# Reordering the front of a fused convolution and attention kernel

## The chip, the cores and the metric

The kernel runs on one core of one Trainium2 chip. All data is float32. The metric is the device time of one launch in microseconds (us); the table below has the median of three runs.

## The reference

The input x has 8 images of 512 channels and 32 x 32 pixels. Cut to what matters:

```python
x = x + block(group_norm(x, 32 groups, eps 1e-5))

def block(x):
    t = silu(bn(conv1x1(x, cv1_w)))                # 512 -> 512 channels
    ys = [t[:, :256], t[:, 256:]]                  # y0 and y1
    for i in range(2):
        yi = ys[-1]
        z = silu(bn(conv3x3(yi, m_cv1_w[i])))      # 256 -> 256
        q, k, v = split(conv1x1(z, m_qkv_w[i]))    # 4 heads of 64
        z = softmax(q^T (k + rw + rh) / 8) applied to v
        ys.append(yi + silu(bn(conv1x1(z, m_cv2_w[i]))))
    return silu(bn(conv1x1(concat(ys), cv2_w)))    # 1024 -> 512
```

The 3x3 convolution is computed in a transformed domain in both directions: filters are turned into "powers" (sums of taps, `make_u`), images into tile inputs (`tiles_in`), products are taken on TensorE, and the results are summed back on VectorE (`conv3x3`).

## The kernel before

**Tiling.** Channels lie on the 128 partitions, so an image of x is four parts (`xts[0]` to `xts[3]`) of 128 x 1024, and the first convolution cv1 has four output blocks of 128 channels: blocks 0 and 1 are y0, blocks 2 and 3 are y1. `Y_ORDER` is 2, 3, 0, 1, because y1 is what the 3x3 convolution needs. Images are worked in pairs; the first pair is called A and B here. Everything that the change touches lies in the front, which is the work ahead of and inside the first 3x3 convolution.

**Norm.** `group_norm_part` is a generator with three steps. The first takes the mean and variance of each channel, either on VectorE (`gn_stats`: two bn_stats and an aggregate for a part) or on ScalarE (`stats_by_act`: a sum by Identity, then a sum of squares by Square, both over 1024 elements). The second averages the mean over groups of 16 channels with a small matmul (`gn_mean`, product gm_ps). The third averages the variance (`gn_rstd`, product gv_ps), raises it to -1/2 with a power on GpSimd (POOL, L700), forms the shift on POOL (L736, L737) and lets ScalarE apply scale and shift in place (L743). Image A is split in two halves: parts 0 and 1 by VectorE, parts 2 and 3 by ScalarE. Image B (`xs_second`) is done by ScalarE as a whole.

**Filters.** `make_u(n, oc, k, area, ...)` makes the powers of one filter block from its nine taps. It goes through i = 2, 0, 1; each i has six VectorE operations of 256 elements (L411 to L416), two ScalarE copies (L409, L410), and for i = 0 and 1 three more VectorE operations of 384 elements ahead (L393 to L399). For output block 0 of the first filter both k go into nine tiles of their own (`first_units`, tag "u", a ring of ten), which the convolution uses directly; when k = 1 is done they are stored to DRAM as nine 512 KB transfers. The two k of block 1 go through twelve half buffers of tag "pt" as eighteen stores of 256 KB. All stores are issued by POOL at L420. The behind_u callback puts some of these steps between applications of B's norm.

**Tile inputs.** `tiles_in(yp, put, is_, ec)` makes the inputs for i = 0, 1 and 2 from y1 of one image. It needs the silus of blocks 2 and 3 (L463). For each i it makes row sums (L520, L524, L527 and L535 to L542), column differences (L556, L557) and the tiles v_in (L559 to L567); POOL writes two edge columns of w_rows (L529, L530). `v_units` places v_in: i = 0 and 1 take the six "pt" buffers, i = 2 takes "v", which held cv1's weights (`w1_first`), and one "x" buffer. Both images share each v_in tile, so a convolution unit starts when both images have written it.

**Order.** Each engine runs its own instructions in one fixed order. A planner forms that order from the order of the program as priority, from dependences and from its own estimates of time, so an instruction written later can come earlier on a free engine. `tc.issue_after(ins)` holds the instructions of a block behind `ins` where both are on the same engine; it makes no wait between engines. Products of cv1 begin before an image's norm is whole: `begin(oc, ks)` runs the parts `ks` of a block and keeps the accumulator in `begun`. There are three accumulators of two banks (`ps_big`), so a fourth block waits until ScalarE's silu has emptied one.

The lines of the front that set this order, before:

```python
begin(Y_ORDER[0], [1])
first = begin(Y_ORDER[1], [0])
with tc.issue_after(first.ins):
    multiplied, _, applied, shifted = next(norm)       # image A, parts 2 and 3
...
s.cv1(w1_of, xs, y0s, Y1[0], Y_ORDER, begun)           # image A
...
s.cv1(w1_of, xs_second, y0s, Y1[1], Y_ORDER)           # image B
```

## Time and profile before

| | us |
|---|---|
| three runs, median (lowest to highest) | 2297.32 (2295.73 to 2301.26) |
| profiled execution, its own time | 2295.83 |
| span in the profile, first to last instruction | 2294.2 |
| TensorE busy over the span | 2217.6 |
| VectorE busy over the span | 1755.7 |
| ScalarE busy over the span | 1090.1 |
| end of the first 3x3 convolution's sums on VectorE | 133.9 |

A timeline line gives the start in us from the span's start, the time taken, the engine (PE is TensorE, DVE VectorE, ACT ScalarE, POOL GpSimd), the line of the kernel, the operation, the tile written and the tiles read, the shape and how many instructions are merged. In brackets is how long the engine stood idle ahead of it, and what ended that. A line of the wait list gives the waiting instruction, what it waited for, and the total, the number and the longest. A line of windows gives busy time by engine, then the granted TensorE clock, the busy share of the DMA engines and GB/s. An f32 matmul appears as two records.

### The profile page before, as it was taken

The page shows a single profiled execution, that of the slowest core. Times are in us where ns is not written, and L with a number is a line of the kernel's source. Part 1 is how long each engine was busy: PE and PEld are TensorE (multiplying, and loading weights), DVE is VectorE, ACT ScalarE, POOL GpSimd, SP SyncE. Part 2 cuts the span into 40 slices and gives each one's busy share as a digit, 9 for nine tenths or more (in the row PEclk, how much of TensorE's full clock was granted, in tenths as well). Part 3 has the DMA queues.
Part 4 walks back from the last instruction along what each step waited for, and adds up shares of the span by engine and source line. Part 5 has one row for each costly group of instructions (what it writes and reads, how often), then busy time and mean ns, then how long its engine had stood idle before and what let it go on. Part 6 is the DMA issues. An engine that isn't in the chain of part 4 may idle for free.

```text
span 2294.2 us, 40531 instructions
## 1 busy us (share of the span) xinstructions
PE 2217.6 (97%) x16338; PEld 1083.3 (47%) x16338; DVE 1755.7 (77%) x2706; ACT 1090.1 (48%) x1342; POOL 208.6 (9%) x417
## 2 busy tenths in 40 slices
PE   6899999999999999999999999999999999999997
PEld 2553437443465443734347443554345733473443
DVE  7887889778858689886857868986894868886742
ACT  7245462545225666365323665445622455335533
POOL 4012200000120000000021000000012000000003
PEclk9999999999999999999999999999999999999999
DMA  9533626321474232612158141442126611251114
GB/s 336 195 108 111 257 76 232 117 75 63 104 221 146 77 123 89 215 44 92 52 150 267 33 160 49 161 132 75 57 73 176 223 46 49 70 196 40 50 28 135
DMA packets 127892, 281.06 MB, mean 123 GB/s; under 512 B 34096, under 2 KB 55324, under 8 KB 126672
## 3 DMA queue, kind: packets, MB, share of 16 engines
q1 hardware_dynamic: 99712, 192.25, 25.4%
q0 software_dynamic: 27984, 86.13, 12.3%
q8 instruction: 131, 2.15, 0.4%
q14 instruction: 65, 0.53, 0.1%
HBM read 210.29 MB, written 68.03 MB: 121 GB/s over the span
## 4 chain that ended last, share of the span: by engine, by line


## 5 line engine op out<-in xcount | busy, mean ns | idle before, releaser
L986 ACT ACTIVATE pt<-l_ps 128x1024 f32<-128x1024 f32 x512 | 495.3, 1023 | 354.5 <-PE l_ps L982 321.8
L1002 DVE TENSOR_TENSOR acc<-acc,pt 128x1024 f32<-128x1024 f32 x384 | 469.6, 1223 | 95.1 <-ACT pt L986 71.3
L1016 PE MATMUL av_ps<-pt,vT 64*64 64x512 f32 x4096 | 489.2, 595 | 11.0 <-DVE z L1024 10.7
L982 PE MATMUL l_ps<-q,kr 64*64 64x512 f32 x4096 | 486.7, 591 | 2.9 <-ACT pt L986 1.9
L1016 PEld LDWEIGHTS av_ps<-pt,vT 64*64 64x64 f32 x4096 | 155.9, 133 | 285.9 <-issue 240.4
L982 PEld LDWEIGHTS l_ps<-q,kr 64*64 64x64 f32 x4096 | 158.1, 133 | 272.9 <-issue 250.6
L611 PEld LDWEIGHTS c_ps<-v_in,u 128*64 128x64 f32 x4320 | 235.7, 137 | 5.3 <-issue 5.3
L611 PE MATMUL c_ps<-v_in,u 128*64 128x128 f32 x4320 | 237.5, 273 | 0.0
L616 ACT COPY c_m<-c_ps 128x512 f32<-128x512 f32 x48 | 28.1, 584 | 185.3 <-PE c_ps L611 108.7
L1214 PE MATMUL m_ps<-z,m_sb 128*128 128x512 f32 x256 | 112.5, 592 | 0.0
L872 PE MATMUL p_ps<-t_z,sq 128*128 128x512 f32 x224 | 106.7, 595 | 3.1 <-DVE c_t L633 3.1
L1000 DVE TENSOR_TENSOR acc<-pt 128x1024 f32<-128x1024 f32 x64 | 77.9, 1217 | 39.2 <-ACT pt L986 39.2
L463 ACT ACTIVATE t<-m_ps,bh,sh 128x512 f32<-128x512 f32 x64 | 46.4, 773 | 75.8 <-PE m_ps L1214 75.8
L872 PE MATMUL p_ps<-z,sq 128*128 128x512 f32 x168 | 80.7, 604 | 0.4 <-ACT m_z L909 0.4
L1284 POOL DMA_DIRECT2D c_out<-in_x_dram x56 | 50.4, 991 | 313.1 <-ACT c_out L463 310.8
L1214 PEld LDWEIGHTS m_ps<-z,m_sb 128*128 128x128 f32 x256 | 48.3, 190 | 58.8 <-issue 56.0
L1088 DVE TENSOR_TENSOR z<-z,rs 128x512 f32<-128x512 f32 x64 | 43.8, 685 | 20.7 <-DMA rs<-r_dram 20.3
L463 ACT ACTIVATE c_out<-cz,bh,sh 128x512 f32<-128x512 f32 x14 | 16.7, 1292 | 90.2 <-DVE cz L1311 90.2
L1024 DVE TENSOR_TENSOR z<-av_ps,z 128x512 f32<-128x512 f32 x64 | 44.0, 688 | 19.7 <-ACT z L1023 19.7
L463 ACT ACTIVATE z<-z,bh,sh 128x512 f32<-128x512 f32 x64 | 47.8, 805 | 21.4 <-DVE z L660 21.4
L490 PE MATMUL ps<-x,w 128*128 128x512 f32 x128 | 56.1, 595 | 0.0
L1334 PE MATMUL x_ps<-t_x,sw 128*128 128x512 f32 x128 | 55.9, 592 | 0.0
(322 smaller groups left out, 3146.2 us busy)
## 6 DMA issues: line engine op xcount, KB each, us to landing
u<-u SPq DMA_DIRECT2D x135, 512.0 KB
sq<-sq SPq DMA_DIRECT2D x42, 384.0 KB
rs<-r_dram SPq DMA_DIRECT2D x118, 128.0 KB
x<-in_x_dram SPq DMA_DIRECT2D x28, 512.0 KB
r_in<-r SPq DMA_DIRECT2D x28, 512.0 KB
y_in<-y SPq DMA_DIRECT2D x28, 512.0 KB
c_out<-in_x_dram POOLq DMA_DIRECT2D x56, 256.0 KB, 5.3
out_dram<-c_out POOLq DMA_DIRECT2D x56, 256.0 KB, 3.7
```

Of the source, the lines that this page charges most:

```text
L463: silued[0] = nc.scalar.activation(dst, src, AF.Silu, scale=sh[:, k : k + 1], bias=bh[:, k : k + 1])
L490: last_product[0] = nc.tensor.matmul(ps[:, half, :], w_of(k), rhs_of(k, half), start=(k == begin), stop=(k == end))
L611: nc.tensor.matmul(to[o], us[cp][:, k, row, c, o], rhs, start=(k == 0), stop=(k == NM - 1),)
L872: nc.tensor.matmul(ps[:, o, :], w[:, o, :], rhs, start=not onto, stop=True, skip_group_check=onto)
L982: nc.tensor.matmul(ps[kh * HD : (kh + 1) * HD, hd, :], kr[r, c, o : o + HD], q[r, c, ts(half, HALF)], start=True, stop=True,)
L986: last_exp[0] = exp = nc.scalar.activation(pt, ps, AF.Exp, scale=SCALE)
L1000: return nc.vector.tensor_tensor(accs[g], pt[0], pt[1], ALU.add)
L1002: ins = nc.vector.tensor_tensor(accs[g], accs[g], pt[i], ALU.add)
L1016: nc.tensor.matmul(avs[g][hd * HD : (hd + 1) * HD, kh, :], vT[r, j, o : o + HD], pt[i][r, hd, :], start=(j == 0), stop=(j == NJ - 1),)
L1214: nc.tensor.matmul(pss[half][:, oc, :], m2_sb[:, n, k, ts(oc, P)], ao[:, k, ts(half, HALF)], start=(k == 0), stop=(k == NM - 1),)
L1284: nc.gpsimd.dma_start(t, rows_of(x, i, at), accum_op=ALU.add)
L1334: nc.tensor.matmul(ps[:, o, :], w[:, c, ts(o, P)], rhs[c], start=(c == 0 and not onto), stop=(c == 1), skip_group_check=onto,)
```

## The change

For image A's second half, the first of two filter steps stays ahead of the variance read and the second goes behind it; block 3 takes both of its first parts before that read. The shift of every such norm is one VectorE operation (`stt`) instead of two on POOL. `make_u` can collect its stores in a list: those of the first unit (`first_stores`) are issued after image B's power and in the program behind the tile inputs, and those of the second filter's beginning (`kept_back`) right after B's power. Image B's statistics use ScalarE for three parts and VectorE for the fourth, and are split in two steps: image A's silus of block 2 stand between the sums and the sums of squares, and those of blocks 3 and 0 behind the squares, ahead of the application of B's norm. Block 1 of image A is computed around B's mean and variance products, and its silus follow the application. Image B's products take parts 0 and 1 of blocks 2 and 3 first. Tile inputs are ordered: image A i = 0 and 1, image B i = 0 and 1, then i = 2 of each. For this pair, i = 2 takes tags "p3" and "p4" instead of "v". The small copies `turn_r` are put behind B's last silu, and in the attention behind an exp.

```diff
--- before.py
+++ after.py
@@ -383,7 +383,7 @@
     def u_new_late():
         return ring([P, 2, 2, P], "u_new")
 
-    def make_u(n, oc, k, area, full=None, new=u_new_late):
+    def make_u(n, oc, k, area, full=None, new=u_new_late, stores=None):
 
         raw = area[:, : 9 * P].rearrange("p (r c o) -> p r c o", r=3, c=3)
         mid = area[:, 9 * P : 15 * P].rearrange("p (r c o) -> p r c o", r=2, c=3)
@@ -417,8 +417,16 @@
             if not full or k == NM - 1:
                 for cp in range(3):
                     dst = u_dram[n][oc][i][cp]
-                    nc.gpsimd.dma_start(dst if full else dst[:, k], full[i, cp] if full else us[cp])
+                    to = (dst, full[i, cp]) if full else (dst[:, k], us[cp])
+                    if stores is None:
+                        nc.gpsimd.dma_start(*to)
+                    else:
+                        stores.append(to)
             yield last
+
+    def put_stores(stores):
+        while stores:
+            nc.gpsimd.dma_start(*stores.pop(0))
 
     NSUM = B * N * NM * NH
     QP = 2 * HALF // P
@@ -465,7 +473,7 @@
             )
             return silued[0]
 
-        shifted, k_added = [None], []
+        shifted, powered, k_added = [None], [None], []
         silu_in, last_product, silued, last_exp, m2_silu = [], [None], [None], [None], [None]
 
         def exp_table():
@@ -697,7 +705,7 @@
             ins = over_groups(ps, dev)
             gr = small.tile([P, n], F32, tag="gr", name="gr")
             read = nc.vector.tensor_scalar(gr, ps, GN_EPS, None, ALU.add)
-            nc.gpsimd.tensor_tensor(gr, gr, mhalf[:, :n], ALU.pow)
+            powered[0] = nc.gpsimd.tensor_tensor(gr, gr, mhalf[:, :n], ALU.pow)
             return gr, ins, read
 
         def stats_by_act(mv, xts):
@@ -707,34 +715,32 @@
             mean = small.tile([P, n], F32, tag="gm", name="mean")
             square = small.tile([P, n], F32, tag="dev", name="square")
 
-            def each(func, to, **kw):
-                for c in range(n):
+            def each(cs, func, to, **kw):
+                for c in cs:
                     bias = {k: v[:, c : c + 1] for k, v in kw.items()}
                     junk = act.tile([P, HW], F32, tag="acc", name="junk", bufs=2)
                     nc.scalar.activation(junk, xts[c], func, accum_out=to[:, c : c + 1], **bias)
 
-            each(AF.Identity, total)
+            each(range(n), AF.Identity, total)
             nc.scalar.activation(mean, total, AF.Identity, scale=-1.0 / HW)
-            each(AF.Square, square, bias=mean)
-            nc.scalar.activation(mv[:, :, 0], total, AF.Identity, scale=1.0 / HW)
-            nc.scalar.activation(mv[:, :, 1], square, AF.Identity, scale=1.0 / HW)
-
-        def group_norm_part(xts, by_act=False, behind=lambda c: None):
+            yield
+            each(range(n), AF.Square, square, bias=mean)
+            nc.scalar.activation(mv[:, :n, 0], total, AF.Identity, scale=1.0 / HW)
+            return nc.scalar.activation(mv[:, :n, 1], square, AF.Identity, scale=1.0 / HW)
+
+        def group_norm_part(xts, by_act=0, behind=lambda c: None):
 
             n = len(xts)
             mv = small.tile([P, n, 2], F32, tag="mv", name="mv", bufs=2)
-            if by_act:
-                stats_by_act(mv, xts)
-            else:
-                for c in range(n):
-                    gn_stats(mv, c, xts[c])
-            yield
+            for c in range(by_act, n):
+                gn_stats(mv, c, xts[c])
+            counted = (yield from stats_by_act(mv, xts[:by_act])) if by_act else None
+            yield counted
             gm, dev, averaged = gn_mean(mv, n, ps_av, "av")
             yield averaged
             gr, multiplied, read = gn_rstd(dev, n, ps_av, "av")
             shift = small.tile([P, n], F32, tag="dev", name="shift")
-            nc.gpsimd.tensor_tensor(shift, gm, gr, ALU.mult)
-            shifted = nc.gpsimd.tensor_scalar(shift, shift, -1.0, None, ALU.mult)
+            stt(shift, gm, -1.0, gr, ALU.mult, ALU.mult)
             for c in range(n):
                 ahead = behind(c)
                 for half in range(NH):
@@ -743,7 +749,7 @@
                         applied = nc.scalar.activation(
                             part, part, AF.Identity, scale=gr[:, c : c + 1], bias=shift[:, c : c + 1]
                         )
-            yield multiplied, read, applied, shifted
+            yield multiplied, read, applied, powered[0]
 
         def group_norm(xts, pieces=1):
 
@@ -1199,8 +1205,8 @@
         def cv1(w_of, xts, y0s, y1, ocs, begun={}):
 
             for oc in ocs:
-                ks = range(NX // 2 if oc in begun else 0, NX)
-                ps = cv1_products(w_of, xts, oc, ks, begun.get(oc))
+                ps, at = begun.get(oc, (None, 0))
+                ps = cv1_products(w_of, xts, oc, range(at, NX), ps)
                 for half in range(NH):
                     dst = y0s[half][:, oc, :] if oc < NM else inner(y1, oc - NM, half)
                     silu(planes(dst), natural(ps[:, half, :]), bn_cv1 + oc)
@@ -1503,17 +1509,19 @@
             nc.sync.dma_start(y1s[half].rearrange("p h c w -> p (h c w)"), y1_dram[b][:, ts(half, NM * HALF)])
         return [[img2(y0s[half]), y1s[half].rearrange("p h c w -> p c h w")] for half in range(NH)]
 
-    def v_units():
+    def v_units(first=False):
 
         vs = {}
         for i in range(NI):
-            if i == 2:
+            if i == 2 and first:
+                both = [act.tile([P, 2, G, 2 * P], F32, tag=tag, name="v_in") for tag in ("p3", "p4")]
+            elif i == 2:
                 both = act.tile([P, 2, 2, G, 2 * P], F32, tag="v", name="v_in")
             for cp in range(3):
                 if i < 2:
                     vs[i, cp] = act.tile([P, 2, G, 2 * P], F32, tag="pt", name="v_in", bufs=6)
                 elif cp < 2:
-                    vs[i, cp] = both[:, cp]
+                    vs[i, cp] = both[cp] if first else both[:, cp]
                 else:
                     vs[i, cp] = act.tile([P, 2, G, 2 * P], F32, tag="x", name="v_in", bufs=NX)
         return vs
@@ -1535,9 +1543,9 @@
                 next(chunk)
         return copied_u[0] if c else None
 
-    first_units = {}
+    first_units, kept_back, first_stores = {}, [], []
     _, _, (_, read, applied, _) = s.group_norm_part(xs[: NX // 2])
-    norm = s.group_norm_part(xs[NX // 2 :], by_act=True)
+    norm = s.group_norm_part(xs[NX // 2 :], by_act=NX // 2)
     for i in (2, 0, 1):
         for cp in range(3):
             first_units[i, cp] = ring([P, NM, 2, 2, P], "u_new")
@@ -1546,11 +1554,13 @@
         for _ in range(5):
             made = next(chunk)
     with tc.issue_after(applied.ins):
-        next(norm)
+        for _ in range(2):
+            next(norm)
     begun = {}
 
     def begin(oc, ks):
-        begun[oc] = s.cv1_products(w1_of, xs, oc, ks, begun.get(oc))
+        ps, _ = begun.get(oc, (None, 0))
+        begun[oc] = s.cv1_products(w1_of, xs, oc, ks, ps), ks[-1] + 1
         return s.last_product[0]
 
     with tc.issue_after(made.ins):
@@ -1559,25 +1569,22 @@
     first = begin(Y_ORDER[0], [0])
     with tc.issue_after(first.ins), tc.issue_after(made.ins):
         averaged = next(norm)
-    chunk = make_u(0, 0, 1, areas[0, 0, 1], first_units)
+    chunk = make_u(0, 0, 1, areas[0, 0, 1], first_units, stores=first_stores)
     with tc.issue_after(averaged.ins):
-        for _ in range(2):
-            made = next(chunk)
+        made = next(chunk)
     begin(Y_ORDER[0], [1])
-    first = begin(Y_ORDER[1], [0])
-    with tc.issue_after(first.ins):
-        multiplied, _, applied, shifted = next(norm)
+    begin(Y_ORDER[1], [0])
+    first = begin(Y_ORDER[1], [1])
+    with tc.issue_after(first.ins), tc.issue_after(made.ins):
+        multiplied, _, applied, powered = next(norm)
     with tc.issue_after(multiplied.ins):
-        begin(Y_ORDER[1], [1])
         begin(Y_ORDER[2], range(NX // 2))
-    with tc.issue_after(made.ins), tc.issue_after(shifted.ins):
+    with tc.issue_after(made.ins), tc.issue_after(powered.ins):
         nc.vector.tensor_scalar(rstd, bnp[:, :, 3], BN_EPS, None, ALU.add)
         nc.gpsimd.tensor_tensor(rstd, rstd, mhalf[:, :NBN], ALU.pow)
-        for _ in range(3):
+        for _ in range(4):
             made = next(chunk)
-    with tc.issue_after(made.ins), tc.issue_after(applied.ins):
-        norm = s.group_norm_part(xs_second, by_act=True, behind=behind_u)
-        next(norm)
+    with tc.issue_after(made.ins):
         for made in chunk:
             pass
     with tc.issue_after(made.ins):
@@ -1587,34 +1594,56 @@
 
         for at in bn_m1:
             made = nc.vector.tensor_scalar(sh[:, at : at + NM], sh[:, at : at + NM], 1 / 36, None, ALU.mult)
-    chunk = make_u(0, 1, 0, areas[0, 1, 0], new=u_new_early)
+    y0s = new_y0()
+    norm = s.group_norm_part(xs_second, by_act=NX - 1, behind=behind_u)
+    with tc.issue_after(applied.ins), tc.issue_after(made.ins):
+        next(norm)
+    s.cv1(w1_of, xs, y0s, Y1[0], Y_ORDER[:1], begun)
+    with tc.issue_after(s.silued[0].ins):
+        counted = next(norm)
+    with tc.issue_after(counted.ins):
+        s.cv1(w1_of, xs, y0s, Y1[0], Y_ORDER[1:3], begun)
+    chunk = make_u(0, 1, 0, areas[0, 1, 0], new=u_new_early, stores=kept_back)
     with tc.issue_after(made.ins):
         for _ in range(4):
             made = next(chunk)
-    with tc.issue_after(made.ins):
+    first = begin(Y_ORDER[3], [0, 1])
+    with tc.issue_after(made.ins), tc.issue_after(first.ins):
         averaged = next(norm)
-        multiplied, _, applied, shifted = next(norm)
-    with tc.issue_after(averaged.ins), tc.issue_after(shifted.ins):
+    first = begin(Y_ORDER[3], [2])
+    with tc.issue_after(made.ins), tc.issue_after(s.silued[0].ins), tc.issue_after(first.ins):
+        multiplied, _, applied, powered = next(norm)
+    with tc.issue_after(powered.ins):
+        put_stores(kept_back)
+    with tc.issue_after(averaged.ins), tc.issue_after(powered.ins):
         for made in chunk:
-            pass
+            put_stores(kept_back)
         for made in make_u(0, 1, 1, areas[0, 1, 1], new=u_new_early):
             pass
-    y0s = new_y0()
-    s.cv1(w1_of, xs, y0s, Y1[0], Y_ORDER, begun)
-    with tc.issue_after(shifted.ins):
+    with tc.issue_after(multiplied.ins):
+        begin(Y_ORDER[3], [3])
+    with tc.issue_after(applied.ins):
+        s.cv1(w1_of, xs, y0s, Y1[0], Y_ORDER[3:], begun)
+    with tc.issue_after(powered.ins):
         keep_y(0, y0s, Y1[0])
     for n in range(N):
         load_m2(n)
     y0s = new_y0()
-    s.cv1(w1_of, xs_second, y0s, Y1[1], Y_ORDER)
-    vs = v_units()
+    begun = {}
+    for oc in Y1S:
+        begun[oc] = s.cv1_products(w1_of, xs_second, oc, range(NX // 2)), NX // 2
+    s.cv1(w1_of, xs_second, y0s, Y1[1], Y_ORDER, begun)
+    vs = v_units(first=True)
+    last = None
     with tc.issue_after(made.ins):
         ecs = [{}, {}]
-        for i in range(NI):
-            for g in range(G):
-                last = s.tiles_in(Y1[g], putter(vs, g), [i], ecs[g])
-    turn_r(0, rw_raw)
-    with tc.issue_after(last.ins):
+        for g, is_ in ((0, (0, 1)), (1, (0, 1)), (0, (2,)), (1, (2,))):
+            with tc.issue_after(last.ins) if last else nullcontext():
+                last = s.tiles_in(Y1[g], putter(vs, g), is_, ecs[g])
+    with tc.issue_after(s.silued[0].ins):
+        turn_r(0, rw_raw)
+    with tc.issue_after(powered.ins):
+        put_stores(first_stores)
         keep_y(1, y0s, Y1[1])
     for (i, cp), u in first_units.items():
         fed["u", 0, 0, i, cp] = u
@@ -1677,7 +1706,7 @@
 
         feed(units(0) + (direct_keys(0) if direct else sqs(0, 0)))
         if p == 0:
-            with tc.issue_after(shifted.ins):
+            with tc.issue_after(powered.ins):
                 first_taps, second_taps = [load_late(0, k, inside(Y2[k])) for k in range(NM)]
         z = new_z()
         t = s.conv3x3(0, vs, u_of(0), z, summed=None if direct else z[:, :, 0], after=last_out)
@@ -1752,7 +1781,8 @@
             raw_1 = load_r(1)
 
             def with_r():
-                turn_r(1, raw_1)
+                with tc.issue_after(s.last_exp[0].ins):
+                    turn_r(1, raw_1)
                 make_r(1)
                 first()
 
```

## The prediction

> **What bounds the kernel now.** The page first: TensorE is busy for 97% of the span, but its first slices read 6, 8, 9, so the loss is at the front. Then the wait lists of VectorE, TensorE and ScalarE between 0 and 160 us, then the timelines of the same engines, then windows.
>
> ```profile
> PE 2217.6 (97%) x16338; PEld 1083.3 (47%) x16338; DVE 1755.7 (77%) x2706; ACT 1090.1 (48%) x1342; POOL 208.6 (9%) x417
> ...
> DVE w_ba L520 <- ACT ypad L463: 8.4, 1, 8.4
> DVE taps L397 <- ACT u_new L410: 1.5, 1, 1.5
> DVE u_new L414 <- DMA u<-u_new: 1.2, 1, 1.2
> DVE dev L692 <- ACT mv L720: 0.9, 1, 0.9
> ...
> 71.18 1.23 DVE L520 SCALAR_TENSOR_TENSOR w_ba<-ypad 128x1024 f32<-128x1024 f32 x1 [8.42 <-ACT ypad L463]
> ```
>
> The reader is to see that VectorE's front is one nearly closed row of work (filter powers, tile inputs, convolution sums) until 133.5 us, and that after 31 us it has one large hole: 62.8 to 71.2, where it waits for image B's first y1. From 71.2 it hardly stops until the convolution ends, while TensorE waits for it (7.7 us at 103.1). So before 133.5 the kernel ends when VectorE ends; after it TensorE leads. Only what fills that hole, or takes VectorE work away, moves the end. Now why image B is late:
>
> ```profile
> 38.89 0.54 POOL L420 DMA_DIRECT2D u<-u_new  x1 [1.55 <-DMA u<-u_new]
> 41.01 0.54 POOL L420 DMA_DIRECT2D u<-u_new  x1 [1.58 <-DMA u<-u_new]
> 41.57 1.27 POOL L700 TENSOR_TENSOR gr<-gr,mhalf 128x4 f32<-128x4 f32 x1
> ...
> 43.79 2.93 ACT L743 ACTIVATE x_second<-x_second,shift,gr 128x512 f32<-128x512 f32 x4 [2.65 <-POOL shift L737]
> ...
> 51.27 2.20 ACT L463 ACTIVATE ypad<-ps,bh,sh 128x512 f32<-128x512 f32 x2
> ...
> 53.52 29.12 PE L490 MATMUL ps<-x_second,w_first 128*128 128x512 f32 x64 [5.19 <-ACT ypad L463]
> ...
> 40.00:60.00 20.00, 13.62 (x28) 5.89 (x29) 17.03 (x40) 15.64 (x26) 13.02 (x23) 0.91 1.02 388
> ```
>
> The power of B's norm is ready to run at 39.6 (its input ends then on VectorE) but stands in POOL's queue behind filter stores that wait for earlier stores to land, and starts at 41.57. ScalarE then applies the norm before it empties image A's products, so TensorE has no free accumulator and starts B at 53.5. The last row says that the DMA engines are full (1.02) at 388 GB/s.
>
> **The change, part by part.**
>
> *Image A's second half.* One filter step instead of two ahead of the variance read takes three VectorE operations (about 1.0 us at 0.335 each) off the path; without stores ahead, the power starts about 1 us earlier again; VectorE's shift (a 0.16 us operation, like L692) replaces 0.67 us of POOL. B's statistics begin on ScalarE about 2 us earlier, near 27. On VectorE nothing gets shorter: it is full from 20.8 to 31.4.
>
> *Image B's statistics.* Part 3 moves to VectorE: two bn_stats and one aggregate, 1.29 + 0.21 = 1.5 us added to the bounding engine; two shifts add 0.4 with their gaps. ScalarE loses 1.04 + 1.13 and their reads.
>
> *When B is ready.* TensorE has 14 pieces (one channel block by one input part, four matmul records of 0.43, so 1.72 us) ahead of B's mean: 12.4 + 14 x 1.72 + about 2 for slow starts is 38.7. One piece more and the variance product: 40.9, which is later than now (39.1). With the power at once (1.27) and the shift, ScalarE applies from about 43.0, hardly earlier than 43.8. The real shift is that the six silus of blocks 2, 3 and 0 (1.1 each) are already done, with statistics and silus filling 27 to 43. Accumulators are free, B's products begin at about 44 on parts 0 and 1, parts 2 and 3 are applied by 49.6, and blocks 2 and 3 (8 pieces, 13.8 us) end at 57.6. Their silus end near 60, against 71.15 now.
>
> *Tile inputs.* Image A's i = 0 and i = 1 now come before B's. A's i = 1 costs 5.1 us (its operations in 77.9 to 89.8, halved, less what belongs to i = 2). Filter powers end at 55.2 now; A then has 6.3 (i = 0) + 1.2 (two L524) + 5.1 = 12.6 us, to about 68. B is ready at 60, so VectorE never waits: the 8.42 goes, with 8 us of margin on B's side. Image B could even slip to 68 at no price.
>
> *The filter waits.* 1.54 + 1.15 + 0.94 = 3.6 us now. I put 2.0 for what replaces them: six stores held until 42.6 mean that the second filter's buffers return a little late (0.5 to 1), and its third step still waits for ScalarE's copies behind the norm (about 1). Bounds 0 and 4. The VectorE shift waits for POOL's power with the queue behind it; the stall is 0 if other filter work stands ahead, 1.3 for the whole power. It lies in these bounds.
>
> *Held stores.* Nine of 512 KB and the six of 256 KB leave POOL's queue ahead of the powers and come after 42.6 with the twelve remaining filter stores (3.1 MB), image A's y (2.1 MB) and two loads of 1.2 MB. POOL pays nothing new: each issue is 0.54 as before. But DMA is nearly idle from about 27 to 42.6 and full after. The risk is the buffers "pt": the inputs of i = 1 take those of the last filter stores. VectorE wants them at about 66. If all 12.7 MB go first at 388 GB/s, they land at 42.6 + 32.7 = 75; if filter stores go first, at about 60. The trace: a 256 KB store lands after 6.3 us median and the longest filter store took 12.5, in a full queue; issued at 57 that is 63.3 or 69.5. The Trainium skill, DMA: Bandwidth & Descriptors, Anatomy of one DMA, speaks for the gentler end: 2.0 us plus bytes over 436 GB/s, an estimate of 2.6 us, landing at 59.6 and waiting nothing. By the rule the sum is 8.1, by the longest row 4.6. The trace decides against the rule while queues are full; I take the median row, with 0.5 us of wait, because program order puts filter stores before the first unit's. Ends 0 and 9.
>
> *TensorE's clock.* Windows after the 5.19 us hole show 0.73, then 0.50 in 54 to 56. The Trainium skill, TensorE: Matmul & The Clock Gate, Part 1, says that an idle window of about 3.4 us halves the clock until a busy one has passed. Without that hole B's products would save some 1.7 us by the rule, making the sum 9.3. I add nothing: VectorE, not B's products, sets the end, and the new wait ahead of the convolution (B's products end near 72, tile inputs of i = 0 at 75.6) would cool the clock again.
>
> *The rest.* Reserving p3 and p4 for i = 2 moves two 384 KB weight loads (now issued at 29.1) behind the convolution; they are wanted late in the first attention, and on SP's queue they then stand behind nothing urgent. Without that cover they cost about 4 us once. The copies of turn_r (0.36 and 0.34) only move on an idle ScalarE. Both at zero.
>
> *Sum on VectorE.* 8.42 − 1.9 (added work) + (3.6 − 2.0) − 0.5 = 7.6 us. All of it arrives at the end, because TensorE leads after 133.5 without waiting for anything on a fixed date. The profiled execution has 2295.83 (span 2294.2), so 2288.2; the median of the three runs shown is 1.5 higher, 2297.32, and 7.6 below that is 2289.7.
>
> **The rivals.** A measurement of this kernel tells 0.3%, 6.9 us, from no change.
> (1) Likeliest, 0.68: the hole is filled, gain 6 to 10; ten is no wait at all in the filters (8.42 + 3.6 − 1.9). About 0.60 of this lies above 6.9 us.
> (2) A transfer takes the hole's place, 0.18: half of the first unit's stores get ahead, the last filter store lands at about 69 to 72, VectorE waits 3 to 6 us on v_in, gain 2 to 5 (2292.3 to 2295.3). For it: DMA shares of 1.02 to 1.05 over 40 us now. Against: the filter stores precede in the program.
> (3) Slower, 0.10: POOL's in-order queue. The edge memsets of w_rows (L529, L530) that image A's i = 1 needs at about 64 stand behind all nine first-unit stores, each of which may wait for an earlier landing, as two do now for 1.6 us each. At the 326 GB/s of the worst full window 12.7 MB take 39 us, to 81.6. The memset then runs 15 to 17 us late; less the 7.6 that is 7 to 10 us slower, about 2306. It decides from a memset at about 72 on; until then there is still a gain.
> (4) More than 10 us, 0.04: TensorE's earlier warmth or better interleaving in the convolution helps too: 2285.
> That the change doesn't do what it says: if VectorE's order still puts A's i = 1 behind B's first tiles, B at 60 is ahead of the end of A's i = 0 at about 63, and the hole is closed all the same; so this is inside (1).
>
> **How the numbers follow.** 2289.7 is case (1). Case (1) alone is 2287.3 to 2291.3; the range reaches into (2) and to the zero-wait end with some spread between runs: 2285.5 to 2297.0. Faster 0.60 + 0.04; same 0.08 + 0.18 + 0.02; slower 0.08.
>
> **What would show it.** The wait of L520 on ypad gone and two L520 groups some 12.6 us apart; VectorE's last convolution operation near 126 instead of 133.5; B's first matmul near 44 and its second ypad silu near 60; L700 for B directly after L699. Wrong: a VectorE wait on DMA or POOL between 55 and 80 (rivals 2, 3), silus of B after 68, or an equal convolution end.

## The result, and the profile after

The changed kernel takes 2292.14 us (median of 8 runs, 2288.88 to 2293.80); the kernel before takes 2297.32 (8 runs, 2294.62 to 2301.33). The ratio is 0.9972, with a 95% interval of 0.9961 to 0.9983: a gain of 5.2 us by the medians, against 7.6 foretold. The profiled executions differ by a little more: 2289.43 against 2295.83, spans 2288.0 against 2294.2. Of the experiments below, one run of kernel 7 was slow (2922.67 us at a mean granted clock of 0.751) and is left out of its ratio.

The busy times hardly move: TensorE 2214.4 us, VectorE 1757.1, ScalarE 1088.3. From VectorE's waits between 4 and 145 us (total, times, longest):

```profile
...
DVE shift L743 <- POOL gr L708: 2.1, 3, 0.9
DVE taps L397 <- ACT u_new L410: 1.5, 1, 1.5
...
```

The 8.4 us wait of the tile input on ypad has left the list. Behind the wait for the first part of x (4.9, and 4.8 before), a new kind stands first: VectorE waits for POOL's power. Its timeline shows where:

```profile
42.93 0.56 DVE L397 SCALAR_TENSOR_TENSOR taps<-taps 128x384 f32<-128x384 f32 x1 [1.52 <-ACT u_new L410]
43.88 0.15 DVE L707 TENSOR_SCALAR gr<-gv_ps 128x4 f32<-128x4 f32 x1
45.39 0.16 DVE L743 SCALAR_TENSOR_TENSOR shift<-gm,gr 128x4 f32<-128x4 f32 x1 [0.90 <-POOL gr L708]
...
57.35 1.22 DVE L528 SCALAR_TENSOR_TENSOR w_ba<-ypad 128x1024 f32<-128x1024 f32 x1
...
70.17 1.22 DVE L528 SCALAR_TENSOR_TENSOR w_ba<-ypad 128x1024 f32<-128x1024 f32 x1
...
127.67 0.42 DVE L668 SCALAR_TENSOR_TENSOR z<-c_r,c_k 128x256 f32<-128x256 f32 x1
```

The two L528 are the first tile operations of image A and image B, 12.8 us apart with no bracket on either. The last line is the end of the convolution's sums. The same two points before, and then the attention's first product, before and after:

```profile
55.19 1.22 DVE L520 SCALAR_TENSOR_TENSOR w_ba<-ypad 128x1024 f32<-128x1024 f32 x1
...
133.51 0.41 DVE L660 SCALAR_TENSOR_TENSOR z<-c_r,c_k 128x256 f32<-128x256 f32 x1
```

```profile
151.24 3.66 PE L982 MATMUL l_ps<-q,kr 64*64 64x512 f32 x32
```

```profile
145.40 3.66 PE L988 MATMUL l_ps<-q,kr 64*64 64x512 f32 x32
```

The sums end at 128.09 instead of 133.92, 5.83 us earlier, and the attention starts 5.84 earlier: what the front won reaches the attention unchanged. It splits like this: the hole is worth 8.42; the filter powers end at 57.35 instead of 55.19, which takes back 2.16; between there and the end of the sums 0.43 more is lost. 8.42 − 2.16 − 0.43 = 5.83. Windows from the end of the filters to the end of the sums, before and after, say what the 0.43 is (VectorE's busy time is the third pair behind the length):

```profile
55.19:133.92 78.73, 66.99 (x647) 48.59 (x646) 69.67 (x146) 20.11 (x27) 5.63 (x20) 0.93 0.53 192
```

```profile
57.35:128.09 70.74, 55.95 (x628) 42.74 (x627) 69.95 (x146) 17.20 (x22) 12.24 (x31) 0.93 0.85 303
```

The same 146 operations keep VectorE busy 0.28 longer, and its idle time without the hole grows by 0.15 (from 0.64 to 0.79). Behind the attention's start the span gains 0.4 more, which no run takes apart.

ScalarE's and TensorE's timelines show image B:

```profile
62.19 2.27 ACT L471 ACTIVATE ypad<-ps,bh,sh 128x512 f32<-128x512 f32 x2 [1.15 <-PE ps L498]
```

```profile
46.45 29.43 PE L498 MATMUL ps<-x_second,w_first 128*128 128x512 f32 x64 [3.17 <-ACT x_second L749]
```

B's first product runs at 46.45 instead of 53.52 and B's y1 is ready at 64.46 (62.19 + 2.27). VectorE asks for it at 70.17: 5.71 us to spare.

### The profile page after: what moved, and what is told of

Same layout as the page of the kernel before. It is cut to its first block, busy times and chain, and to the rows that moved or that the text cites. A ratio compares the mean times of both kernels' runs of the same rounds, so it can differ in the third digit from the quotient of the medians.

```text
span 2288.0 us, 40522 instructions
## 1 busy us (share of the span) xinstructions
PE 2214.4 (97%) x16338; PEld 1081.6 (47%) x16338; DVE 1757.1 (77%) x2712; ACT 1088.3 (48%) x1338; POOL 205.3 (9%) x411
## 4 chain that ended last, share of the span: by engine, by line
## 5 line engine op out<-in xcount | busy, mean ns | idle before, releaser
L878 PEld LDWEIGHTS p_ps<-t_z,sq 128*128 128x128 f32 x224 | 39.2, 192 | 35.8 <-issue 35.8
```

Of the source, the lines that this page charges most:

```text
L878: nc.tensor.matmul(ps[:, o, :], w[:, o, :], rhs, start=not onto, stop=True, skip_group_check=onto)
```

## The experiments

Each kernel has 5 to 21 runs, timed beside the kernel before. "End" is the end of the convolution's sums in the profile, and "filters" is when VectorE starts image A's tile inputs. The times of one kernel spread by 5 to 10 us from run to run, so end and filters are the finer measure; but each comes from one profiled execution, and they too differ between executions, by up to 1.3 us (kernels 1 and 12 below).

| kernel | filters, us | end, us | median, us (before in the same call) | ratio, 95% |
|---|---|---|---|---|
| before | 55.19 | 133.92 | | 1 |
| changed | 57.35 | 128.09 | 2292.14 (2297.32) | 0.9972, 0.9961 to 0.9983 |
| 1 tile order alone | 53.90 | 128.15 | 2292.60 (2297.92) | 0.9976, 0.9969 to 0.9983 |
| 2 old tile order | 57.40 | 130.62 | 2293.78 (2297.92) | 0.9984, 0.9977 to 0.9991 |
| 3 shift on POOL | 57.30 | 128.43 | 2291.54 (2297.92) | 0.9978, 0.9967 to 0.9988 |
| 4 B's statistics on ScalarE | 56.22 | 127.91 | 2292.31 (2297.92) | 0.9972, 0.9961 to 0.9984 |
| 5 second filter's stores not held | 57.30 | 128.68 | 2293.51 (2299.05) | 0.9974, 0.9966 to 0.9983 |
| 6 as 5, shift on POOL | 58.28 | 129.71 | 2295.08 (2299.05) | 0.9982, 0.9975 to 0.9989 |
| 7 as 6, B's statistics on ScalarE | 59.00 | 130.10 | 2297.20 (2299.05) | 0.9989, 0.9982 to 0.9995 |
| 8 as 7, copies ahead of silus | 56.45 | 127.23 | 2291.01 (2299.05) | 0.9970, 0.9957 to 0.9982 |
| 9 as 8, copies inside the norm | 53.61 | 126.42 | 2291.41 (2297.67) | 0.9963, 0.9949 to 0.9976 |
| 10 no store held | 57.24 | 128.61 | 2291.30 (2297.67) | 0.9973, 0.9964 to 0.9982 |
| 11 four more pieces ahead of B's silus | 57.50 | 128.81 | 2292.10 (2297.67) | 0.9973, 0.9963 to 0.9984 |
| 12 as 9, B's y stores on SP | 54.18 | 125.70 | 2288.54 (2299.00) | 0.9954, 0.9940 to 0.9967 |

**Which part does it (1, 2).** The theory: the order of the tile inputs closes the hole; the rival: B has to come earlier. Kernel 1 is the kernel before with only this:

```
-        for i in range(NI):
-            for g in range(G):
-                last = s.tiles_in(Y1[g], putter(vs, g), [i], ecs[g])
+        last = None
+        for g, is_ in ((0, (0, 1)), (1, (0, 1)), (0, (2,)), (1, (2,))):
+            with tc.issue_after(last.ins) if last else nullcontext():
+                last = s.tiles_in(Y1[g], putter(vs, g), is_, ecs[g])
```

> The kernel before, with the new order of the tile inputs alone (image A i = 0 and 1, image B i = 0 and 1, then i = 2 of each). Theory: VectorE sets the end of the front, and its 8.42 us hole is closed either by making image B earlier or by giving VectorE the 5.1 us of image A's i = 1 to do in it. Then this one edit leaves a hole of 3.3 us, the convolution's sums end 5.1 us earlier than 133.9 (at about 128.8), and the time falls by about 5 us, to 2292. Rival: the gain comes from image B's earlier start; then the order alone gives less than 1.5 us.

Its timeline of VectorE:

```profile
53.90 1.22 DVE L520 SCALAR_TENSOR_TENSOR w_ba<-ypad 128x1024 f32<-128x1024 f32 x1
...
70.21 1.22 DVE L520 SCALAR_TENSOR_TENSOR w_ba<-ypad 128x1024 f32<-128x1024 f32 x1 [3.17 <-ACT ypad L463]
```

B is nearly as late as before (it is used at 70.21, 71.18 before), yet the end is the changed kernel's within 0.06 us. VectorE reaches B at 67.04 and waits 3.17, so the hole shrinks by 5.25, close to the 5.1 expected.

The filters' earlier end, 53.90 instead of 55.19, is not the edit's: up to there VectorE, ScalarE and POOL have the order of before. In this execution POOL waited once for a store to land (1.22 us) where it had waited twice (1.55 and 1.58), so B's power ran earlier than the 41.57 of before:

```profile
40.33 1.05 POOL L700 TENSOR_TENSOR gr<-gr,mhalf 128x4 f32<-128x4 f32 x1
```

With the filters and the B of before, VectorE would reach B at 68.33, wait until 71.18 and, with this run's 57.94 us behind it, end at 129.1: by this estimate the order alone is worth 4.8 us at the end of the sums, 5.8 as profiled. The changed kernel has no wait at B, but its filters end 3.45 later than here, 2.16 later than before. So on top of the order, all the rest of the change removes 3.17 and pays between 2.16 and 3.45 for it. By the medians of the times there is nothing between the two (5.3 us against 5.2).

Kernel 2 is the changed kernel with the removed lines back.

> The changed kernel with the tile inputs in the order of before (i = 0 of A and B, i = 1 of A and B, i = 2 of A and B). Theory: image B's silus end at 64.5, ahead of the end of A's i = 0 on VectorE at 64.8, so no hole opens and the convolution's sums end at 128.1 as in the changed kernel (within 0.5 us). Rival: the order is what closes the hole; then a wait on ypad of 4 to 5 us returns and the gain is gone.

```profile
64.25 1.29 DVE L532 TENSOR_TENSOR w_ec<-ypad 128x512 f32<-128x512 f32 x2 [2.54 <-ACT ypad L471]
```

An early B alone closes most of the hole, not all: the planner set B's w_ec ahead of the rest of A's i = 0 and met it at 61.7, with B ready only at 64.2. The end is 2.53 later than with the new order, which is this wait; the expectation, no hole, was missed. Either half alone gives more than half of the 5.83 (3.30 here, 4.8 to 5.8 in kernel 1); they don't add.

**Where the missing gain went (3, 4).** The theory: VectorE's queue stands behind POOL's power for the shift (0.90 at 45.39, 0.59 at 23.56), and behind the statistics of B's part 3 (1.5 us of work). Kernel 3 gives the shift back to POOL:

```
-            stt(shift, gm, -1.0, gr, ALU.mult, ALU.mult)
+            nc.gpsimd.tensor_tensor(shift, gm, gr, ALU.mult); powered[0] = nc.gpsimd.tensor_scalar(shift, shift, -1.0, None, ALU.mult)
```

> The changed kernel with the shift of the three split norms on POOL again (two POOL operations, POOL's queue still free of stores). Theory: the shift on VectorE costs the bounding engine 2.1 us of waiting for POOL's power and 0.3 us of work, and buys nothing, because image B has 5 us to spare; so the sums of the convolution end 1.5 to 2.4 us earlier than 128.1 (part may return as a longer wait for ScalarE's copies). Rival: the earlier shift is worth its wait; then the end is 0.5 us or more later.

```profile
52.06 0.42 DVE L414 SCALAR_TENSOR_TENSOR u_new<-taps 128x256 f32<-128x256 f32 x1 [1.50 <-DMA u<-u_new]
```

The shift's waits are gone, and the filters end at 57.30 all the same: VectorE is earlier at 52 and waits 1.50 for a buffer whose held-back store has not landed (0.21 in the changed kernel, at 52.10). The end, 128.43, is no earlier either: the theory of 1.5 to 2.4 us fell. Kernel 4 computes all of B's statistics on ScalarE:

```
-    norm = s.group_norm_part(xs_second, by_act=NX - 1, behind=behind_u)
+    norm = s.group_norm_part(xs_second, by_act=NX, behind=behind_u)
```

> The changed kernel with all four parts of image B's statistics on ScalarE. Theory: 1.5 us of VectorE work goes, image B becomes some 2 us later (silus end near 66.5) and is still ahead of VectorE at about 68.5; the sums of the convolution end 1 to 1.5 us earlier than 128.1. Rival: ScalarE's later copies hold the filter powers (the 1.5 us wait of L397 grows by as much as 2 us), and nothing or a loss of up to 1 us comes out.

Of 1.5 us taken off VectorE, 1.13 shows at the end of the filters and 0.18 at the end of the sums. The wait for ScalarE's copies grew from 1.52 to 1.78 and the mean's product became a wait of 0.88; behind the filters two waits of 0.46 and 0.48 came up (at 78.16 and 115.88).

**Taking the next wait away (5, 6, 7).** If the DMA buffer took over, stores that are not held should free it. Kernel 5:

```
-    chunk = make_u(0, 1, 0, areas[0, 1, 0], new=u_new_early, stores=kept_back)
+    chunk = make_u(0, 1, 0, areas[0, 1, 0], new=u_new_early)
```

> The changed kernel, in which the six stores of the second filter's beginning are issued as they are made instead of after image B's power. VectorE's and ScalarE's orders are the same. Theory: the held stores give the pt buffers back late, but in the changed kernel that is hidden behind VectorE's stalls for POOL's power; so only the 0.2 us wait on DMA goes and the convolution's sums end at 127.9 instead of 128.1. Rival: the stores in POOL's queue delay the power again and B's norm comes later; with B's spare time that costs nothing at the end either, but the power must then start later than 44.2.

Kernel 6 adds the edit of 3 to it, kernel 7 the edit of 4 as well.

> As the kernel with the stores unheld, and the shift on POOL too. Theory: with the shift on POOL alone VectorE's 2.1 us of stalls came back as waits of 1.5 and 0.3 us for the held stores' buffers; with both edits neither wait is there, the filter powers end 1.5 to 2.2 us earlier than 57.3 and the convolution's sums end at 126.0 to 126.6. Rival: something else takes the wait again (ScalarE's copies, an image B that is late), and the end stays within 0.7 us of 128.1.

> As before, and all of image B's statistics on ScalarE. Theory: 1.4 us less work on VectorE; the sums of the convolution end at 124.7 to 125.3, and the time is 3 us below that of the changed kernel, near 2289. Rival: the wait of L397 for ScalarE's copies grows by what is saved, and the end is that of the kernel without this edit.

In kernel 5 the DMA wait of 0.21 is gone and the filters still end at 57.30. From VectorE's timeline in kernel 6:

```profile
54.49 0.56 DVE L397 SCALAR_TENSOR_TENSOR taps<-taps 128x384 f32<-128x384 f32 x1 [2.00 <-ACT u_new L410]
```

Neither the power nor the DMA is waited for, and the filters end later, at 58.28. In the place of the three stalls for the power (0.62, 0.68 and 0.93 in kernel 5) stand waits for ScalarE's copies (L409, L410): 0.60 at 16.19, 0.72 at 28.41 and this one of 2.00, beside the old one (1.56 at 43.33). The copies stand in ScalarE's queue behind image A's silus and B's norm, and with two POOL operations behind the power ScalarE begins B's norm at 46.88 instead of 45.83. Kernel 7 loads ScalarE more and is worst: 59.00, end 130.10. Both missed their expected ends, and the theory that the power's wait was the cost fell here; what remained to try was ScalarE's order.

**Moving the copies (8, 9, 12).** Kernel 8 is kernel 7 with the copies of the second filter's i = 0 ahead of A's silus of blocks 3 and 0:

```
-    with tc.issue_after(counted.ins):
-        s.cv1(w1_of, xs, y0s, Y1[0], Y_ORDER[1:3], begun)
     chunk = make_u(0, 1, 0, areas[0, 1, 0], new=u_new_early)
...
         for _ in range(4):
             made = next(chunk)
+    with tc.issue_after(counted.ins), tc.issue_after(copied_u[0].ins):
+        s.cv1(w1_of, xs, y0s, Y1[0], Y_ORDER[1:3], begun)
```

> As before, and ScalarE makes the two copies of the second filter's i = 0 ahead of image A's silus of blocks 3 and 0 instead of behind them. Theory: L397 no longer waits (1.3 to 1.8 us); the sums of the convolution end at 123.3 to 124, and the time is about 4 us below that of the changed kernel, 2288. Image B's silus must still end ahead of VectorE's tile inputs of A (about 66); rival: they do not, since the copies and the norm's application stand in each other's way on ScalarE, and a wait on ypad opens again.

One edit of order, no work less, and the filters end 2.55 earlier than in kernel 7, the sums 2.87. (The expected 123.3 to 124 counted on kernels 6 and 7 and was missed.) A wait of 1.72 at 52.65 was left, on copies behind B's norm application. Kernel 9 puts the first four steps of the next filter between the applications of parts 0 and 1 and of parts 2 and 3 (`second` is that filter's `make_u`; only these lines are shown):

```
     def behind_u(c):
         if c == 2:
             for _ in range(3):
                 next(chunk)
+            for _ in range(4):
+                next(second)
```

> The kernel before this one (ScalarE copies of the second filter's i = 0 ahead of image A's silus) still has one VectorE wait of 1.72 us at L397 near 52.65, on ScalarE copies that stand behind the norm application of B's parts 2 and 3. Here the first four steps of the next filter are put between the applications of parts 0-1 and 2-3, so their copies stand earlier in ScalarE's order. Theory (the front's end is VectorE's work plus waits for ScalarE copies): that wait falls below 0.3 us, the filter powers end near 54.8 to 55.2 instead of 56.45, the convolution sums end at 125.5 to 126.3 instead of 127.23, the time is 1 to 1.7 us lower than that kernel's. Rival (image B's products are now what counts): B's norm application is about 2 us later, B's first silus end after 65, and the convolution sums end at 127 or later; no gain.

```profile
49.81 0.56 DVE L397 SCALAR_TENSOR_TENSOR taps<-taps 128x384 f32<-128x384 f32 x1 [0.40 <-ACT u_new L410]
...
76.85 0.69 DVE L564 TENSOR_TENSOR w_d<-w_rows 128x512 f32<-128x512 f32 x1 [1.77 <-POOL w_rows L537]
```

The filters end 2.84 earlier than in kernel 8, more than expected, but the sums only 0.81: a new wait of 1.77 on POOL's edge memset, and 0.3 at L640. POOL's timeline says why:

```profile
76.11 0.53 POOL L1497 DMA_DIRECT2D y<-y_half  x1 [8.22 <-ACT y_half L471]
76.64 0.18 POOL L537 MEMSET w_rows<- 128x32 f32 x1
```

This is rival (3) of the prediction in small: the memset stands in POOL's queue behind a store, here of B's y, that waits for B's silu. Kernel 12 sends B's three y stores through SP's queue; the orders of the other engines are those of kernel 9:

```
+            (nc.sync if b == 1 else nc.gpsimd).dma_start(y0_dram[b][half], y0s[half])
...
+        (nc.sync if b == 1 else nc.gpsimd).dma_start(y1_dram[b], inside(y1))
```

> The kernel with both copies moved (the second filter's i = 0 copies ahead of image A's silus, the next filter's first steps between the applications of B's norm) still has a VectorE wait of 1.77 us at 76.85, on POOL's edge memset of w_rows. POOL is in order, and that memset stands behind the store of B's first y0 half, which is issued at 76.11, when ScalarE has emptied the products. Here the three stores of B's y go to SP's queue; TensorE's, VectorE's and ScalarE's orders stay the same. Theory (the wait is nothing but POOL's order): it goes, the convolution sums end at 124.5 to 125.2 instead of 126.42, the attention's first product at 142 to 142.6 instead of 143.72, the time is about 1.3 to 1.8 us lower, some 7 to 8 us below the kernel before. Rival (SP's queue only takes the wait over): the filter loads behind the stores on SP come late, TensorE waits for them in the convolution's second half, and the sums end at 126 or later.

The wait on POOL is gone. The end, 125.70, moved by 0.72 and missed the expected range: the filters ended 0.57 later in this execution (L397's ypad waits summed to 1.7 instead of 0.9), and 0.6 instead of 0.3 was waited at L640. No wait for SP's queue shows up in its place. The attention starts at 144.68, later than kernel 9's 143.72; the last section says why. At 0.9954 this kernel beats the one before; against the changed kernel (0.9972) the intervals overlap, so it is ahead by its median, not beyond doubt.

**Does B, or do the stores, still count (10, 11)?** Kernel 10 is the changed kernel with no store held: both `stores=` arguments left out.

> The changed kernel with every filter store issued as soon as it is made, as before; the orders of TensorE, VectorE and ScalarE stay those of the changed kernel. Theory A (the delay of B's power behind stores is covered: B has 5.7 us of margin, and only the shift on VectorE feels it): B's power runs 1 to 2.5 us later, B's first silus end at 65 to 67, VectorE's wait at the shift grows from 0.9 to 1.5 to 3, the convolution sums end at 128.3 to 130 instead of 128.09, the time is 0 to 2 us above that of the changed kernel. Theory B (holding the stores back is what keeps the gain): with full queues the power is 5 us or more late, VectorE stalls as long at the shift, the convolution sums end at 132 or later and the gain is gone.

```profile
44.35 1.21 POOL L708 TENSOR_TENSOR gr<-gr,mhalf 128x4 f32<-128x4 f32 x1 [0.45 <-DVE gr L707]
```

B's power is 0.15 later than in the changed kernel (44.20), and what POOL waits for ahead of it is VectorE's read, not a store. The end is 0.52 later, by a wait of 0.7 on the w_rows memset. In these two executions, holding the stores back is worth half a microsecond at the end; the times don't show it.

Kernel 11 gives TensorE four more pieces ahead of B's silus; part 1 counts three times in two blocks, so the output is another:

```
-        begun[oc] = s.cv1_products(w1_of, xs_second, oc, range(NX // 2)), NX // 2
+        begun[oc] = s.cv1_products(w1_of, xs_second, oc, [0, 1, 1, 1]), NX // 2
```

> The changed kernel with four pieces of TensorE work more ahead of image B's first silus: of the products of B's blocks 2 and 3, those of input part 1 are added two times more (part 1 counts three times in these two blocks, which changes the output). That is 16 matmul records of 0.43 us, 6.9 us, so B's silus of those blocks end near 71.3 instead of 64.46. Theory (VectorE sets the end and does not need B before 70.17): VectorE waits about 1.2 us at the first tile operation of B, the convolution sums end at 129 to 129.8 instead of 128.09, and the time is about 1 to 1.7 us higher. Rival (when B is ready sets the end): the convolution sums end 6.9 us later, near 135, and the time is 6 to 7 us higher.

```profile
46.48 34.60 PE L498 MATMUL ps<-x_second,w_first 128*128 128x512 f32 x80 [2.36 <-ACT x_second L749]
...
67.39 2.27 ACT L471 ACTIVATE ypad<-ps,bh,sh 128x512 f32<-128x512 f32 x2 [1.15 <-PE ps L498]
...
70.32 1.22 DVE L528 SCALAR_TENSOR_TENSOR w_ba<-ypad 128x1024 f32<-128x1024 f32 x1
```

B is ready at 69.66, 5.2 later instead of 6.9 (the clock, below), and VectorE uses it at 70.32 without a wait. The end moves by 0.72: 0.15 from the filters, and waits of 0.18 for POOL and 0.60 for ScalarE's copies of the convolution's products (L640). Of B's 5.7 us to spare, 5.2 could be used up without a wait for B.

## Why the prediction was right, and where not

**The hole: right, but its cause only in half.** The 8.42 us went, and what was won reaches the attention whole. But the prediction let "B ready at 60" carry it, and said that the hole would close even if VectorE's order didn't change. Kernel 2 has that case: 2.54 us of wait remain. Kernel 1 shows that the order alone gives 4.8 to 5.8 of the 5.8, with B nearly as late as ever.

**The range: wide.** 2285.5 to 2297.0 reaches from almost no gain to 12 us. The case that it called likeliest, 6 to 10 us, did not come: 5.2 by the medians and 5.8 at the end of the sums lie just below it. Nor did a gain above 6.9 us, to which it gave 0.64.

**When B is ready: too early by 4.5 us, at no price.** B's products were put at 44 and its y1 at 60; measured 46.45 and 64.46. TensorE's part was right: the mean's product, put at 38.7 (its own terms sum to 38.5), runs at 38.95, and the variance product, put at 40.9, at 41.09.

```profile
41.09 0.28 PE L688 MATMUL gv_ps<-dev,gmat 64*64 64x4 f32 x4
```

The power does follow its input at once now (L707 at 43.88, L708 at 44.20; 2.1 us lay between them before). But the read L707 comes 2.5 us after the product's end: it stands on VectorE behind L397, which waits 1.52 for ScalarE's copies. The prediction took the power's queue as the delay and did not follow the read back into VectorE's queue. Most of the other 2 us is a lower clock (below). Kernel 11 shows that such a delay of B costs no wait.

**The filter waits: the term that was mis-sized.** The prediction had 1.9 of added work and 3.6 − 2.0 of waits saved, 0.3 net lost; measured are 2.16. Windows say which, from the end of the same operation (the variance of image A's first half, L692 and L700) to the end of the filters, before and after:

```profile
20.84:55.19 34.35, 27.12 (x66) 11.67 (x67) 29.84 (x85) 28.42 (x54) 21.66 (x33) 0.92 1.03 386
```

```profile
21.23:57.35 36.12, 32.95 (x83) 14.26 (x83) 31.66 (x91) 28.89 (x51) 13.61 (x19) 0.95 0.52 185
```

VectorE's busy time grew by 1.82, so the 1.9 was right. Its idle time fell by 0.05 only (4.51 to 4.46), where 1.6 was expected, although the DMA share fell from 1.03 to 0.52. Named waits fell from 3.63 to 3.22 (0.59, 1.52, 0.90, 0.21); small gaps ate the rest. "The shift's stall is 0 if other filter work stands ahead" was the wrong end of its bound: 1.49 of the 3.22 are shifts. Another 0.39 was lost ahead of 21 us: the first part of x came 0.10 later, and a third shift, at 10.83, which the prediction left out of its two, cost 0.78 and saved 0.50 of a later wait for a copy. 0.39 + 1.82 − 0.05 = 2.16.

Kernels 3, 6 and 7 then show that removing the stalls brings nothing by itself: other waits take their place, for a store's buffer in kernel 3, for ScalarE's copies in 6 and 7. What did bring the filters' end forward was ScalarE's order (kernels 8 and 9). Both have the shift on POOL and the stores not held as well; the new order by itself, on the changed kernel, was not run.

**The v_in wait: 0.5 taken, 0 found.** No tile input of i = 1 waits for DMA, so rival (2) did not occur; the median row was nearer than the longest. In its place 0.43 went elsewhere (longer operations and small gaps), so that the two numbers agree is chance.

**The clock: right to add nothing.** B's products lost 1.75 us to a lower clock in the changed kernel (29.43 for 64 records, against 34.60 × 64 / 80 = 27.68 in kernel 11; the granted clock from 46 to 50 us is 0.64 and then 0.50, in kernel 11 it is 1.00). That is close to the 1.7 that the prediction estimated from the window of about 3.4 us in the Trainium skill, TensorE: Matmul & The Clock Gate, Part 1. But the saving did not come: a wait of 3.17 had taken the place of the 5.19, and 29.12 became 29.43. It is off the path, as kernel 11 shows, where B comes 5.2 us later still and VectorE does not wait for it.

**The slower rival.** In the changed kernel no memset was waited for. Its mechanism showed in kernels 5 to 7 and 9 to 11, at 0.2 to 1.8 us, not 15.

So 7.6 was foretold and 5.8 came at the end of the sums: the forecast had 1.86 too little lost in the filters and 0.07 too much behind them. What was not tried is the new place of the two weight loads by itself; the attention's start moves with the sums to 0.01 us, so no cost shows up to there.

## What to carry to other kernels

When an in-order engine waits for one input and holds other work that is ready, change its order first: here that edit alone did what the whole rearrangement of the front did. A wait on the path that is removed is worth only the distance to the next one on that engine; look for the engine that most of them lead back to (here ScalarE, whose queue held two copies of 0.4 us behind silus and a norm), and move its small, wanted operations forward. Before hurrying a producer, delay it on purpose: if the end doesn't move, it isn't what to hurry.

## What the runs showed of the hardware

TensorE's granted clock can fall after a wait, and the length of that wait alone does not decide it. In kernels 9 and 12 TensorE waits 2.05 us at the same place, behind the same 1.98 us of products, ahead of the same 12 products. First kernel 9, then kernel 12, each with the window of 4 us around it (the granted clock is the third figure from the end of the window's row):

```profile
124.63 5.39 PE L498 MATMUL ps<-z,w_qkv 128*128 128x512 f32 x12 [2.05 <-DVE c_t L641]
```

```profile
124.00:128.00 4.00, 3.37 (x8) 1.63 (x9) 2.90 (x10) 3.06 (x5) 0.00 (x0) 1.00 0.01 4
```

```profile
123.91 7.06 PE L498 MATMUL ps<-z,w_qkv 128*128 128x512 f32 x12 [2.05 <-DVE c_t L641]
```

```profile
124.00:128.00 4.00, 4.00 (x6) 1.76 (x7) 1.66 (x6) 3.25 (x5) 0.00 (x0) 0.59 0.00 0
```

Kernel 9 goes on at full clock. Kernel 12 has 0.59 over these 4 us (0.50 from 124 to 127) and loses 1.67 us. That is all of what it won on VectorE and 0.95 more: 0.72 earlier at the end of the sums, 0.96 later at the attention. At this place no other kernel lost anything, with waits of 2.05 to 2.61. Ahead of B's products, waits of 1.29 to 2.36 cost nothing, and from 2.60 on all of them lowered the clock. So 2.60 us (kernel 3, ahead of B's products) and 2.61 (kernel 7, at the place above) again part:

```profile
46.20 29.43 PE L498 MATMUL ps<-x_second,w_first 128*128 128x512 f32 x64 [2.60 <-ACT x_second L749]
```

```profile
128.31 5.39 PE L498 MATMUL ps<-z,w_qkv 128*128 128x512 f32 x12 [2.61 <-DVE c_t L641]
```

The Trainium skill, TensorE: Matmul & The Clock Gate, Part 1, has the clock fall after an idle window of about 3.4 us. By that neither a wait of 2.05 nor one of 2.60 would cost anything; kernels 12 and 3 show that they can. The page also calls the window free-running, not tied to the work; whether its place decides between such pairs, no run here shows. For a forecast it means that waits of 2.0 to 2.6 us in this kernel cost either nothing or 1.7 us, and that an end moved by less than that can be hidden by it.

Two smaller ones. A power on POOL of 128 x 4 takes 1.15 us in the changed kernel, and VectorE stood idle for 0.90 of it. And in the changed kernel the DMA share is 1.01 from 56 to 84 us, yet neither TensorE nor VectorE waits for a transfer there: busy DMA engines cost these two nothing in that stretch.
